# Gate and up of the last four blocks: six of eleven column groups by two levels of seven products

## The chip, the cores and the metric

One NeuronCore of a Trainium2 chip runs the whole kernel in one launch. The metric is device microseconds from start to end of the launch; the kernel before takes 1817.15 us (median of three runs, 1816.91 to 1817.16). Everything is float32. TensorE (PE in the profile) multiplies matrices into PSUM, which has eight banks of 128x512 floats; VectorE (DVE) and ScalarE (ACT) read and write PSUM and SBUF; GpSimd (POOL) works on SBUF alone here; SyncE's queue (SPq) issues nearly all DMAs, in program order.

## The reference

```python
x = x + xattn(layernorm(x), ctx, mask, mask, Wq, bq, Wk, bk, Wv, bv)   # 16 heads, per batch
n = layernorm(x)                       # x is [16, 256, 512]: 4096 rows of 512
gate = n @ lut[gate_idx].T             # 512 -> 1376
up   = n @ lut[up_idx].T               # 512 -> 1376
h    = silu(gate) * up
x    = x + h @ lut[down_idx].T         # 1376 -> 512
```

## The kernel before

The kernel has three stages: attention, then gate and up, then down. The change is in the second and at the start of the third.

**Tiling.** The 4096 rows are eight blocks of 512 rows. `xTs[n]` holds block n, normalized and turned: 512 features in four chunks of 128 by 512 rows. `wg` and `wu` hold gate and up, four chunks of 128 features by 1376 columns. The columns are eleven groups `o` of 128, the last of 96 (`NO` is 11). Two blocks make a pair `p`, 0 to 3.

**A unit** (`unit(p, o)`, L942 to L1006) makes gate and up of one column group for one pair by one level of a seven-product scheme (Winograd's form of Strassen's): the two rows of the left matrix are gate and up, its two columns the halves of the features; the two columns of the right one are the blocks of the pair. Each of the seven products, pa, pe, pa, pb, pa, pc, pd in the order of issue, is two matmuls of 128x512 (the two chunks of a half), so a unit has 14 where eight plain products would take 16. Sums that a scheme like this needs are made ahead: of the weights by `combine_w` into `sw` and in place in `wu`, of the rows by `combine_x` (L848) into `xe` and in place in `xTs`. Sums of the products are made in PSUM: ScalarE copies a bank (`copied`, L961), and later products are added onto the bank and onto its copy. Three products are joined with others by VectorE from PSUM (L989 hb, L993 w, L1003 ha); ScalarE applies Silu to `sg` (L983) and `w` (L994), GpSimd multiplies hb by w (L995), and SyncE's queue stores both parts to DRAM (`store_h`). The addition ha is put off into the next unit (`hold`).

**The order of units** (L1009) is written out: `gate_up` does column group 0 of pairs 0 and 1 plainly, then come 20 units of pairs 0 and 1 and all 22 of pairs 2 and 3. Within a unit, places are left for VectorE's other work: `hooks` run at three places of a unit (loads of rows, their statistics, normalizing, turning, `combine_x`; `turn_blocks` sets them), and `fill(ns)` adds to a budget and emits as many of the table look-ups that are still to be done (`todo`: the rest of the weights, `combine_w`, then the down weights `wd`) as fit into it, by planned costs. The fills of one unit sum to 9300 planned ns.

**Down** (`down7`, L1182) takes a block's h in four quarters, again by seven products q1 to q7 of five or six matmuls of 128x256 each, on four PSUM banks (`ps_b`). Its weight sums t2, t3, t4 and `wl` are made once, by VectorE, in `before_down` (L1097), mixed with the sums of block 0's h (`combine_h(0)`: s1, s2, an in-place difference, s4). Two steps of it run in the last unit, three after it, and one after each of the first additions of the first `down7`, where q6 needs s2 and t2, q7 needs t3, q5 needs `wl`. Every `down7` also loads two tiles of x (`load_x2`, L1188) that its second addition (L1222) and later ones need. Block 0's h is loaded in unit (3, 2), half of block 1's in unit (3, 5); the pools of the gate and up stage are then closed, and at L1236 the other half of block 1 and block 2 are loaded. For later blocks, block n + 2 is loaded when block n is done.

Of the kernel before, what the change touches and what calls it, by code (L numbers as in the profile page):

```python
# [9 lines left out]
F32 = mybir.dt.float32  # L10
I32 = mybir.dt.int32
AF = mybir.ActivationFunctionType
ALU = mybir.AluOpType
# [6 lines left out]
def kernel(  # L20
# [34 lines left out]
    nc = tc.nc  # L55
    P = 128
    B, C, T = x.shape
# [10 lines left out]
    NH = T // P  # L68
# [107 lines left out]
    xTs = {}  # L176
# [7 lines left out]
    def load_x2(k):  # L184
        x2s[k] = rpool.tile([P, T], F32, tag="x2", name=f"x2t_{k}", bufs=4)
        nc.sync.dma_start(x2s[k], x2_d[k])
        return x2s[k]
# [617 lines left out]
    with ExitStack() as ffn:  # L805
# [7 lines left out]
        )  # L813
        first = ffn.enter_context(ExitStack())
        sp = first.enter_context(tc.tile_pool(name="ffns", bufs=1))
        f1 = first.enter_context(tc.tile_pool(name="ffn1", bufs=3))

# [9 lines left out]
        def store_h(n, o, ht, rows):  # L827
            nc.sync.dma_start(hds[n][o, :rows, :], ht[:rows])
# [83 lines left out]
        def fill(ns):  # L912

            room[0] = min(room[0] + ns, 8000.0)
            while room[0] > 0:
                took, op = next(todo, (0, None))
                if op is None:
                    break
                op()
                room[0] -= took  # L920
# [21 lines left out]
        def unit(p, o, hooks):  # L942
# [27 lines left out]
            if held:  # L970
                held.pop()()
            pe = bank("pe", ps_f, "ae")
            product(pe, sw[:, 0], t1, onto=False)
            p5 = rpool.tile([P, 4 * P], F32, tag="us1", name=f"p5_{p}_{o}", bufs=1)[:rows]
            nc.scalar.copy(p5, pe)
            fill(2000)
            product(pa, sw[:, 1], xe[:, 1])
# [15 lines left out]
            v.tensor_tensor(w, pc, p5, ALU.add)  # L993
            nc.scalar.activation(w, w, AF.Silu)  # L994
            nc.gpsimd.tensor_tensor(hb, hb, w, ALU.mult)  # L995
            store_h(2 * p + 1, o, hb, rows)
            product(pd, a22, xe[:, 2])
            hooks[2]()
            fill(1700)

# [4 lines left out]

            held.append(hold)  # L1006


        order = [(p, o) for o in range(1, 8) for p in range(2)]  # L1009
        order += [(p, o) for p in range(2) for o in range(8, NO)]  # L1010
        order += [(p, o) for p in range(2, 4) for o in range(NO)]
        hooks = defaultdict(list)

        def turn_blocks(n, at):

            k = 4 * n

            def step(i):
                if i:
                    turn2(k + i - 1)  # L1020
                if i < 8:
                    norm2(k + i)
                    room[0] -= 550
                if i + 3 < 8:
                    load_x2(k + i + 3)
                if i == 8:
                    for _ in combine_x(n // 2):
                        room[0] -= 1230

            for i in range(3):  # L1030
                hooks[divmod(at - 1, 3)].append(lambda i=i: load_x2(k + i))
            for i in range(9):
                hooks[divmod(at + i, 3)].append(lambda i=i: step(i))

        turn_blocks(4, 3 * order.index((1, 8)) - 1)
        turn_blocks(6, 3 * order.index((2, 5)))
        for i in range(8):
            for n, at in ((4, 8), (6, 15)):
                hooks[at + i, 0].append(lambda k=4 * n + i: load_x2(k))
                hooks[at + i, 1].append(lambda k=4 * n + i: (stats2(k), fill(-850)))  # L1040
        for n, at in ((4, 16), (6, 23)):
            hooks[at, 0].append(lambda n=n: [fn() for fn in rstd2(n, n + 2)] and fill(-2300))
# [26 lines left out]
        for i in range(4):  # L1069
            hooks[0, min(i, 2)].append(lambda: (next(second, None), fill(-1230)))  # L1070

        def run(fns):
            for fn in fns:
                fn()
# [6 lines left out]
        lo, hi = slice(0, 2 * P), slice(2 * P, 4 * P)  # L1081
        wl, wh, wz = wd[:, 0:HO], wd[:, HO : 2 * HO], wd[:last_rows, NO - 1]
        h_parts = {}

        def load_part(n, o, t):
            full = min(t.shape[1], NO - 1 - o)
            nc.sync.dma_start(t[:, 0:full], hds[n][o : o + full].rearrange("o p t -> p o t"))
            if full < t.shape[1]:
                nc.sync.dma_start(t[:last_rows, full, :], hds[n][NO - 1, :last_rows, :])

        def part_of(t, i):
# [43 lines left out]
        for i, (p, o) in enumerate(order):  # L1135
            if p < 2 and o in (5, 8):
                while o not in ready:
                    next(todo)[1]()
            if (p, o) == (3, 2):

                h_parts[0] = [(j, xpool.tile([P, NH, 4 * P], F32, tag="xT", name=f"h0_{j}")) for j in (0, 4)]
                h_parts[0][1] = (4, h_parts[0][1][1][:, 0 : HO - 4])
                h_parts[0].append((HO, xep.tile([P, 3, 2, 4 * P], F32, tag="xe", name="h0_2")
                                   .rearrange("p a b t -> p (a b) t")))
                for part in h_parts[0]:
                    load_part(0, *part)
            if (p, o) == (3, 5):
                for _, op in todo:
                    op()
                h_parts[1] = [(0, look[:, 0:HO])]  # L1150
                load_part(1, *h_parts[1][0])
            if (p, o) == order[-1]:
                pre = before_down()
                hooks[i, 1].append(lambda: next(pre))
                hooks[i, 2].append(lambda: next(pre))
            unit(p, o, [lambda i=i, j=j: run(hooks.pop((i, j), ())) for j in range(3)])
        held.pop()()
        first.close()
        hp = ffn.enter_context(tc.tile_pool(name="ffnh", bufs=2))

        def load_high(n):
            h_parts[n].append((HO, hp.tile([P, NO - HO, 4 * P], F32, tag="hh", name=f"hh_{n}")))
            load_part(n, *h_parts[n][-1])

        def load_h(n):
            low = look[:, 0:HO] if n % 2 else hp.tile([P, HO, 4 * P], F32, tag="hl", name=f"hl_{n}", bufs=1)
            h_parts[n] = [(0, low)]
            load_part(n, 0, low)
            load_high(n)

# [11 lines left out]
        def down7(n, t, pre=iter(())):  # L1182
# [4 lines left out]
            first_t, second_t = slice(t * P, (t + 1) * P), slice((t + 2) * P, (t + 3) * P)  # L1187
            xrs = [load_x2(4 * n + t), load_x2(4 * n + t + 2)]  # L1188

# [45 lines left out]

        load_high(1)  # L1236
        load_h(2)
        for _ in range(3):
# [3 lines left out]
        for n in range(nblocks):  # L1242
            if n:
                down7(n, 0)
            if n + 1 < nblocks:
                for _ in combine_h(n + 1):
                    pass
            down7(n, 1)
            h_parts.pop(n)
            if n == 0:  # L1250
                new_e(0)
            elif n + 2 < nblocks:
                load_h(n + 2)

# [45 lines left out]
```

## Time and profile before

| | us |
|---|---|
| median of three runs | 1817.15 |
| the profiled execution | 1816.28 |
| its span, first to last instruction | 1814.5 |
| TensorE busy | 1783.5 |
| VectorE busy | 1340.0 |
| ScalarE busy | 870.8 |
| GpSimd busy | 435.8 |
| the 42 units, first to last matmul | about 1009.7 to 1525.5 |
| down | about 1525.5 to 1814.5 |

The granted TensorE clock is 0.996 of full speed over the span. A float32 matmul of this kernel shows as two matmul records. Neighbouring records overlap, so a mean duration of one (592 ns for 128x512) is longer than the time from one start to the next, and the rate of TensorE is read from starts. "Idle before" in the profile is time in which an engine had nothing to do just before an instruction, and the name behind the arrow is what ended it.

### The profile page before, as it was taken

To read this page: it belongs to the slowest core of one execution; us is meant where nothing else is said; L and a number is where in the kernel's file an instruction comes from. 1 tells how busy PE (TensorE), PEld (TensorE's weight loads), DVE (VectorE), ACT (ScalarE), POOL (GpSimd) and SP (SyncE) were. 2 spreads that over 40 slices of the span, in tenths; PEclk is the share of its full clock that TensorE was granted. 3 is DMA by queue.
4 is the path that set the end of the run, shared out by engine and by line. 5 is a ranking of instruction groups with operands and counts; after the bars stand their busy time and mean duration, and the time that the engine had idled before them with its cause. 6 is when DMAs were issued, how large, how long until landed. Compare 5 with 4: busy or idle time off the path is not lost.

```text
span 1814.5 us, 28718 instructions
## 1 busy us (share of the span) xinstructions
PE 1783.5 (98%) x10982; PEld 836.5 (46%) x10982; DVE 1340.0 (74%) x1886; ACT 870.8 (48%) x1651; POOL 435.8 (24%) x425
## 2 busy tenths in 40 slices
PE   8999999999999999999999999999999998899999
PEld 4333333333333333333344444444444444788887
DVE  6898999989998999998887788887873113453352
ACT  2777777777777777777775222233232221000000
POOL 4334333434334443444322111101111010000000
PEclk9999999999999999999999999999999999999999
DMA  6445533333434245444332111232221323233531
GB/s 188 132 145 155 155 105 125 121 116 93 127 121 128 89 127 153 143 133 123 111 103 87 60 58 68 76 119 73 70 91 38 109 75 117 69 132 125 178 132 59
DMA packets 118937, 201.09 MB, mean 111 GB/s; under 512 B 21892, under 2 KB 24072, under 8 KB 118800
## 3 DMA queue, kind: packets, MB, share of 16 engines
q1 hardware_dynamic: 114528, 196.21, 34.1%
q0 software_dynamic: 3168, 1.86, 0.5%
q8 instruction: 87, 1.43, 0.3%
q10 hardware_dynamic: 1104, 1.19, 0.2%
q14 instruction: 50, 0.41, 0.1%
HBM read 135.83 MB, written 58.10 MB: 107 GB/s over the span
## 4 chain that ended last, share of the span: by engine, by line
PE 91%; DVE 3%; DMA 2%; ACT 1%; SPq 0%; issue 0%; DVEq 0%; ACTq 0%
PE pa L490 15%; PE pv L537 12%; PE pa L956 12%; PE q L1199 12%; PE pb L498 11%; PE pb L956 4%; PE pd L956 4%; PE pc L956 4%; PE pe L956 4%; PE pv L413 3%; PE pq L413 3%; PE pk L413 3%; DMA x2t<-x 2%; PE pgu L930 2%; DVE nm L506 1%; PE q L1204 1%
## 5 line engine op out<-in xcount | busy, mean ns | idle before, releaser
L506 DVE TENSOR_REDUCE nm<-pa 128x2 f32<-128x1024 f32 x512 | 602.1, 1217 | 84.9 <-PE pb L498 79.7
L510 ACT ACTIVATE pt<-pb 128x512 f32<-128x512 f32 x1024 | 530.3, 603 | 105.9 <-PE pb L498 104.4
L490 PE MATMUL pa<-kp,qp 32*128 32x512 f32 x2048 | 514.2, 616 | 6.5 <-DVE nm L506 3.8
L498 PE MATMUL pb<-qp,kp 32*128 32x512 f32 x2048 | 517.4, 617 | 0.0
L490 PEld LDWEIGHTS pa<-kp,qp 32*128 32x128 f32 x2048 | 177.7, 184 | 200.4 <-DVE nm L506 152.8
L537 PE MATMUL pv<-pt,va 128*32 128x512 f32 x2048 | 246.2, 598 | 0.0
L498 PEld LDWEIGHTS pb<-qp,kp 32*128 32x128 f32 x2048 | 209.9, 183 | 73.2 <-issue 41.3
L995 POOL TENSOR_TENSOR hb<-hb,w 128x512 f32<-128x512 f32 (+1 forms) x42 | 57.2, 1362 | 465.4 <-ACT w L994 448.2
L989 DVE TENSOR_TENSOR hb<-pa,p 128x512 f32<-128x512 f32 (+1 forms) x42 | 29.0, 689 | 148.3 <-ACT pd L963 148.3
L537 PEld LDWEIGHTS pv<-pt,va 128*32 128x32 f32 x2048 | 53.4, 109 | 173.1 <-ACT pt L510 97.1
L1218 ACT COPY q<-q 128x256 f32<-128x256 f32 x16 | 6.0, 372 | 265.1 <-PE q L1199 265.1
L542 ACT COPY us<-pv 128x512 f32<-128x512 f32 x128 | 75.0, 586 | 94.6 <-PE pv L537 94.6
L521 POOL DMA_DIRECT2D qp<-mx x64 | 38.3, 599 | 312.5 <-DVE mx L520 295.1
L549 POOL TENSOR_TENSOR us<-us,us 128x512 f32<-128x512 f32 x64 | 82.3, 1286 | 15.1 <-ACT us L542 15.0
L956 PE MATMUL pa<-xe,sw 128*128 128x512 f32 (+1 forms) x168 | 79.9, 598 | 2.1 <-ACT pb L963 2.1
L956 PE MATMUL pb<-xT,wg 128*128 128x512 f32 (+1 forms) x168 | 79.9, 598 | 0.0
L956 PE MATMUL pc<-xT,sw 128*128 128x512 f32 (+1 forms) x168 | 79.0, 592 | 0.0
L956 PE MATMUL pa<-xT,wg 128*128 128x512 f32 (+1 forms) x168 | 78.9, 592 | 0.0
L956 PE MATMUL pd<-xe,wu 128*128 128x512 f32 (+1 forms) x168 | 78.9, 592 | 0.0
L956 PE MATMUL pa<-xe,wu 128*128 128x512 f32 (+1 forms) x168 | 78.9, 592 | 0.0
L956 PE MATMUL pe<-xT,sw 128*128 128x512 f32 (+1 forms) x168 | 78.9, 592 | 0.0
L429 POOL TENSOR_TENSOR natk<-natk,mb 128x512 f32<-128x512 f32 x31 | 40.9, 1318 | 145.9 <-ACT natk L426 140.6
(227 smaller groups left out, 2405.2 us busy)
## 6 DMA issues: line engine op xcount, KB each, us to landing
x2t<-x SPq DMA_DIRECT2D x96, 256.0 KB
kp<-kd SPq DMA_DIRECT2D x62, 256.0 KB
qp<-qd SPq DMA_DIRECT2D x62, 256.0 KB
h<-hb SPq DMA_DIRECT2D x38, 256.0 KB
h<-ha SPq DMA_DIRECT2D x38, 256.0 KB
hh<-h SPq DMA_DIRECT2D x7, 1280.0 KB
rb<-rd SPq DMA_DIRECT2D x32, 256.0 KB
xr<-in_x_dram SPq DMA_DIRECT2D x32, 256.0 KB
```

The lines of the kernel that those rows point to most:

```text
L413: nc.tensor.matmul(ps[32 * j : 32 * j + 32], weights(o, slice(first + 32 * j, first + 32 * j + 32)), moving(o), start=(o == 0), stop=(o == ...
L429: nc.gpsimd.tensor_tensor(t, t, mb, ALU.mult)
L490: nc.tensor.matmul(pa[:, jj, :], qps[ua % 4][at, ca * P : (ca + 1) * P], kps[ua % 4][at, :], start=True, stop=True,)
L498: nc.tensor.matmul(pb, kps[ub % 4][at, cb * P : (cb + 1) * P], qps[ub % 4][at, :], start=True, stop=True,)
L506: nc.vector.tensor_reduce(nms[ua][:, 2 * half : 2 * half + 2, ca], pa, AX.X, ALU.max, negate=True)
L510: nc.scalar.activation(pts[sb][:, j, :], pb, AF.Exp)
L537: nc.tensor.matmul(ps[32 * j : 32 * j + 32, :], va[:, at : at + 32], pt[:, j, :], start=(i == 0), stop=(i == 1),)
L542: nc.scalar.copy(us[u, half], ps)
L549: nc.gpsimd.tensor_tensor(a, a, b, ALU.add)
L956: nc.tensor.matmul(ps, a[:, h, at], b[:, h, :], start=h == 0 and not onto, stop=h == 1, skip_group_check=onto,)
L995: nc.gpsimd.tensor_tensor(hb, hb, w, ALU.mult)
L1199: nc.tensor.matmul(ps, a(o)[:, at], b[:, o, :], start=o == 0, stop=o == HO - 1 and not more,)
```

## The change

For pairs 2 and 3, units are left only for column groups 0, 1, 2, 3 and 10, ten units in place of 22. Column groups 4 to 9 are taken two at a time, (4, 5), (6, 7), (8, 9), for both pairs at once, by a second level of the same scheme (`quads`). For each **column pair** there are seven **items**, one for each product of the first level, in the order `seq`: 1, 2, 6, 7, 4, 3, 5. In an item, the left matrix has the two column groups and the two chunks of 128 features, the right one the two chunks and the two pairs, and it is done by seven **products** of one matmul of 128x512 each. They are issued in the order f6, f2, f5, f7, then the f1 of the next item, f3, f4. Four results of 128x512 come out of an item (for two column groups and two pairs), and each is added to running sums in SBUF.

- `second_x(i)` makes the sums of rows of item i once, four VectorE instructions of 128x512; it runs for items 1, 2, 6 ahead of the first column pair and for 7, 4, 3, 5 in items 1, 2, 6, 7 of it (`tails`).
- `second_w`, by `factors`, makes the sums of weights for each item, four instructions of 128x128, one item ahead.
- Per item ScalarE copies three banks. `share_e` reads the bank pe (one buffer) twice, `result` reads the others.
- Running sums are in buffers of tags that the units used (us0, x2, us1, rb, xr); sums of rows and the first loads of h lie in parts of `sw`, `look`, `wg` and `wu` that are no longer needed.
- In the units, Silu of w, GpSimd's multiplication and the store of hb are put off into the next unit (`hold_w`), the last fill is 2200 instead of 1700, `combine_x` is spread over two hooks, and statistics and turning of pairs 2 and 3 run earlier.
- The loads of h for blocks 0 and 1 are issued in the last column pair, together with the x tiles of block 0's two `down7`; only the low half of block 1 is loaded after it. `before_down`'s first two steps run in the last item. Block 2 is loaded after block 0 is done. `combine_h(n + 1)` runs between the additions of the second `down7` of block n rather than ahead of it.

```diff
@@ unit
             if held:
-                held.pop()()
+                held.pop(0)()
...
             nc.scalar.copy(p5, pe)
+            if held:
+                held.pop(0)()
             fill(2000)
...
             v.tensor_tensor(w, pc, p5, ALU.add)
-            nc.scalar.activation(w, w, AF.Silu)
-            nc.gpsimd.tensor_tensor(hb, hb, w, ALU.mult)
-            store_h(2 * p + 1, o, hb, rows)
             product(pd, a22, xe[:, 2])
             hooks[2]()
-            fill(1700)
+            fill(2200)
...
-            held.append(hold)
+            def hold_w():
+                nc.scalar.activation(w, w, AF.Silu)
+                nc.gpsimd.tensor_tensor(hb, hb, w, ALU.mult)
+                store_h(2 * p + 1, o, hb, rows)
+
+            held.extend([hold, hold_w])
...
-        order += [(p, o) for p in range(2, 4) for o in range(NO)]
+        order += [(p, o) for p in range(2, 4) for o in (0, 1, 2, 3, NO - 1)]
...
                 if i == 8:
-                    for _ in combine_x(n // 2):
+                    combining.append(combine_x(n // 2))
+                if i >= 8:
+                    for _ in range(2):
+                        next(combining[-1])
                         room[0] -= 1230
...
-        turn_blocks(6, 3 * order.index((2, 5)))
+        turn_blocks(6, 3 * order.index((2, 0)) - 1)
...
+        def second_x(i):
+            b1, b2 = rows_in(2, i), rows_in(3, i)
+            t2, t3, t4 = t_of[i]
+            v.tensor_tensor(t3, b2[:, 1], b2[:, 0], ALU.subtract)
+            v.tensor_tensor(b2[:, 0], b2[:, 0], b1[:, 0], ALU.subtract)
+            v.tensor_tensor(t2, b2[:, 1], b2[:, 0], ALU.subtract)
+            v.tensor_tensor(t4, b1[:, 1], t2, ALU.subtract)
...
+        def second_w(i, at, at2, ring):
+            a = weights_of(i)
+            s1, s2, s4 = (ring[:, j * P : (j + 1) * P] for j in range(3))
+            v.tensor_tensor(s1, a[:, 0, at2], a[:, 1, at2], ALU.add)
+            v.tensor_tensor(s2, s1, a[:, 0, at], ALU.subtract)
+            v.tensor_tensor(a[:, 0, at2], a[:, 0, at], a[:, 0, at2], ALU.subtract)
+            v.tensor_tensor(s4, a[:, 1, at], s2, ALU.subtract)
...
+            def begin(j, f):
+                pa = bank(j, "a")
+                product(pa, f[1], onto=False)
+                return pa, copied(j, "b", pa)
...
+                else:
+                    if shared:
+                        v.tensor_tensor(tmp, ps, tmp, ALU.add)
+                        v.tensor_tensor(r, tmp, r, ALU.add)
+                        nc.gpsimd.tensor_tensor(w, tmp, w, ALU.add)
+                    else:
+                        v.tensor_tensor(w, ps, w, ALU.add)
+                        v.tensor_tensor(r, ps, r, ALU.add)
+
+                    def end():
+                        nc.scalar.activation(w, w, AF.Silu)
+                        nc.gpsimd.tensor_tensor(r, r, w, ALU.mult)
+                        store_h(5 + 2 * pair, o, r, P)
+
+                    late.append(end)
...
+            for j, (q, o, i) in enumerate(work):
...
+                nf = factors(j + 1) if j + 1 < len(work) else None
+                product(pa, f[6])
+                pc = copied(j, "c", pa)
+                if late:
+                    late.pop(0)()
+                product(pb, f[2])
+                result(q, o, i, 0, pb, tmps[0])
+                pe = bank(j, "e")
+                product(pe, f[5], onto=False)
+                share_e(q, i, pe, tmps)
+                product(pa, f[7])
+                pd = copied(j, "d", pa)
+                if nf:
+                    na, nb = begin(j + 1, nf)
+                result(q, o, i, 1, pa, tmps[1])
+                product(pc, f[3])
+                result(q, o, i, 2, pc, tmps[2])
+                product(pd, f[4])
+                for _ in range(3):
+                    if late:
+                        late.pop(0)()
+                for fn in tails.get((q, i), ()):
+                    fn()
+                result(q, o, i, 3, pd, tmps[3])
...
+        for fn in held:
+            fn()
+        second_x(2)
+        second_x(6)
+        pre = before_down()
+        last_q = len(pairs_of_o) - 1
+        quads(extra, {
+            (0, 1): [lambda: second_x(7)], (0, 2): [lambda: second_x(4)],
+            (0, 6): [lambda: second_x(3)], (0, 7): [lambda: second_x(5)],
+            (last_q, 1): [lambda: load_high(1)], (last_q, 2): [lambda: load_high(0)],
+            (last_q, 7): [lambda: load_low(0)],
+            (last_q, 3): [lambda: xrs_of.update({(0, t): load_xrs(0, t) for t in range(2)})],
+            (last_q, 5): [lambda: next(pre), lambda: next(pre)],
+        })
...
-        load_high(1)
-        load_h(2)
+        load_low(1)
         for _ in range(3):
             next(pre)
         down7(0, 0, pre)
...
-            if n + 1 < nblocks:
-                for _ in combine_h(n + 1):
-                    pass
-            down7(n, 1)
+            pre = combine_h(n + 1) if n + 1 < nblocks else iter(())
+            down7(n, 1, pre)
+            for _ in pre:
+                pass
```

## The prediction

> **What bounds the kernel now.** I read the page first, then busy time by stage, then TensorE's waits, then the timelines where it waits.
>
> ```profile
> PE 1783.5 (98%) x10982; PEld 836.5 (46%) x10982; DVE 1340.0 (74%) x1886; ACT 870.8 (48%) x1651; POOL 435.8 (24%) x425
> ...
> PE   8999999999999999999999999999999998899999
> ...
> DVE  6898999989998999998887788887873113453352
> ```
>
> TensorE works nearly without a break, and VectorE has room only from slice 31 on: the look-ups end there. By stage (PE, PEld, DVE, ACT, POOL):
>
> ```profile
> 1009.70:1526.00 516.30, 514.21 (x1244) 227.72 (x1243) 326.97 (x582) 156.18 (x268) 56.30 (x42) 1.00 0.22 74
> 1526.00:1562.00 36.00, 23.78 (x102) 19.75 (x101) 20.91 (x25) 0.74 (x2) 0.89 (x1) 0.86 0.51 175
> 1562.00:1814.50 252.50, 248.16 (x1147) 217.01 (x1145) 102.87 (x182) 5.21 (x14) 0.00 (x0) 1.00 0.35 117
> ```
>
> The units run at TensorE's rate (2.1 us idle of 516.3); the start of down loses 12.2 of 36. The waits that do so:
>
> ```profile
> PE q L1199 <- DVE wd L1106: 9.9, 1, 9.9
> ...
> PE pa L956 <- ACT pb L963: 2.1, 1, 2.1
> ...
> PE q L1199 <- DVE wu L1105: 2.0, 1, 2.0
> ```
>
> The first is a DMA's doing:
>
> ```profile
> 1534.23 1.62 SPq L186 DMA_DIRECT2D x2t<-x  x2
> ...
> 1545.48 0.42 DVE L1211 TENSOR_TENSOR q<-q,x2t 128x256 f32<-128x256 f32 x1 [10.37 <-DMA x2t<-x]
> 1545.83 1.48 DVE L1106 TENSOR_TENSOR wd<-wd 128x1280 f32<-128x1280 f32 x1
> ...
> 1547.46 3.83 PE L1199 MATMUL q<-wd,wg 128*128 128x256 f32 x10 [9.86 <-DVE wd L1106]
> ```
>
> The x tiles queue behind three loads of h (4.2 MB, 1530.2 to 1545.4, 277 GB/s); VectorE waits for them in order, and `wl`, which q5 needs, comes behind.
>
> **Matmuls.** One unit's pa starts at 1381.27 and the next one's at 1393.29: 12.02 us for 14 matmuls, 0.859 each. Twelve units (168) become 21 items of seven (147): 21 x 0.859 = **18.0 us less**, if TensorE stays the bound. An item lasts 6.01 us, a column pair 42.1.
>
> **VectorE in the column pairs.** Joining a 128x512 PSUM bank with SBUF takes 0.69 us (hb and w, 689 and 688 ns), two SBUF operands 0.69 too (ob_xr<-ob_xr,x2t, 692). 128x256 takes 0.424; the line through both puts 128x128, which no such addition here shows, at 0.29. Bounds are 0.21 (the 128x128 copy L357) and 0.42; I take 0.29. An item then costs: `factors` 4 x 0.29 = 1.16; item 1 two results on VectorE (the rest are ScalarE copies), 2.5 in all; items 2, 6, 7, 4, 3 six, 5.3; item 5 eight, 6.7. A column pair is 2.5 + 5 x 5.3 + 6.7 = 35.7 against TensorE's 42.1: it fits. The first also bears four `second_x` (4 x 0.69 = 2.75 each): 46.7, and two more, 5.5, stand just ahead. It doesn't fit.
>
> How far VectorE may lag follows from the order. f5 of the next item overwrites the one-buffer pe, so it waits for `share_e`, 3.2 us into VectorE's item; f6 waits for s2, 0.6 into it. Time 0 is the end of the last unit's matmuls. f1 goes at once, but f6 waits for ScalarE's copy (0.2 from matmul to copy, 0.57 the copy, as for pb, pc, pd): item 1 starts at 1.7, **0.8 lost**. VectorE finishes ha at 0.9, `second_x(2)` and `(6)` at 6.7, item 1 with `second_x(7)` at 12.0, then 8.0 us an item: item 2 at 20.0, 6 at 28.0, 7 at 36.0, item 4 at 41.3. TensorE starts item 2 at 7.7, unhindered; item 6 at 13.7, where ScalarE's Silu of item 2's third result (ready at 16.6) stands ahead of the copy that f7 needs, **1.6** lost; item 7 loses **0.25** at f5 (23.0 to 23.3); item 4 loses 1.05 at f6 and 0.95 at f5; item 3 the same: **4.0**. Item 5 then starts at 43.8.
>
> **Item 5.** Its third result goes VectorE, GpSimd's addition (1.27, L995), Silu (0.63), and only then can ScalarE copy for the next item's f7. Unlagged, the third sum is ready 6.1 us into the item, GpSimd after VectorE's next addition at 8.1, Silu 8.8, copy 9.4: 0.85 later than f7 wants. In the first pair VectorE lags some 2 us more: **3.0** lost, and 0.2 from GpSimd in item 3; in the second pair I take **1.3**, with GpSimd's interference from item 4. After the third no item follows. Item 1 (2.5 us of VectorE) lets it catch up. All told **9.9 and 1.3 us back**.
>
> **GpSimd against VectorE.** An addition with both inputs in SBUF suffers when GpSimd works:
>
> ```profile
> 1524.56 2.62 DVE L1125 TENSOR_TENSOR wg<-wg,h 128x1024 f32<-128x1024 f32 x2
> ...
> 1525.49 1.40 POOL L995 TENSOR_TENSOR hb<-hb,w 96x512 f32<-96x512 f32 x1 [10.74 <-ACT w L994]
> ```
>
> The two should take 1.22 + 0.42; they take 2.62, one microsecond more. A column pair has ten GpSimd instructions (it had one per unit) against VectorE's `factors`, `second_x` and r additions. For one PSUM input, the 512 reductions L506 in attention, with GpSimd busy 38% of that time, range only from 1193 to 1233 ns, so I charge the results nothing. [...]
>
> **Start of down.** In the last item VectorE has eight results, `before_down`'s first two (1.48 each), then t2's two and the difference before q6 and q7. Without collisions q6 waits until 8.4 us after the last matmul, though q1 and q2 end at 4.75 (3.6), and q7 2.4 for t3: 6.0 idle. With GpSimd's remaining five instructions taking turns with VectorE's five, 10.4. I take 9.2, nearer the collision that the row shows. The x tiles now come three items earlier (18 us ahead, against 11.2 to land at their worst), so the 9.9 us wait goes. 12.2 becomes 9.2: **3.0 less** (1.8 to 6.2). The loads: high halves of 1.5 MB in items 1 and 2 (5.4 us each at 277 GB/s), block 0's low half three items before the end, block 1's about 8 us after it and needed some 25 us later: hidden by the matmuls of item 7 to 5 and of the first `down7`; uncovered, 5 us. Block 2 now loads between blocks as blocks 3 to 7 did, where TensorE lost nothing outside the tail.
>
> **Units.** The 2.1 us wait arose so:
>
> ```profile
> 1254.75 1.23 DVE L856 TENSOR_TENSOR xe<-xT,xe 128x1024 f32<-128x1024 f32 x1
> ...
> 1257.29 0.68 DVE L993 TENSOR_TENSOR w<-pc,p 96x512 f32<-96x512 f32 x1
> 1258.06 0.63 ACT L994 ACTIVATE w<-w 96x512 f32<-96x512 f32 x1 [7.12 <-DVE w L993]
> 1258.60 0.57 ACT L963 COPY pb<-pa 128x512 f32<-128x512 f32 x1
> ...
> 1259.22 2.83 PE L956 MATMUL pa<-xe,sw 128*128 128x512 f32 x4 [2.09 <-ACT pb L963]
> ```
>
> Four `combine_x` in one lump made w late, Silu waited, the next unit's copy behind it. With Silu held and the lump split, **2.1 less**. The held store of hb now goes out some 6 us into a unit, not 1.5, and the statistics' x loads queue behind it on SyncE: VectorE may wait about 2 us once, then lags by it, which `hold`'s slack (w must be done before p5 is written, 5 us later) covers; if not, 2 us. VectorE's look-ups must now end in 30 units: planned, 82 (eight weight pieces) + 140 (eleven of wd) + 15 (`combine_w`) + 46 (rows) - 9 (done ahead) = 274 us; at 9.3 a unit 29.5 (the trace's last look-up ends at 1369.9, unit 30), at 9.8 unit 28.0. VectorE, 10.2 of 12.0 us per unit now (42.6 of 50), goes to about 10.7. So nothing is left to flush ahead of the last unit, and these moves cost nothing.
>
> **Sum**: -18.0 + 9.9 + 1.3 - 3.0 - 2.1 = -11.9 us. The profiled execution, 1816.28 (span 1814.5 and 1.8 around it), would become 1804.4; the median lies 0.87 above it, so 1805.2, told as **1805**. With the bounds (128x128 at 0.21 or 0.42, a lag cost of 6 to 14, the start of down from 6 to 12) its own range is 1797 to 1813.
>
> **Rivals.** *VectorE hides all of it*: TensorE may run further ahead than I allow. For: two of three column pairs need only 35.7 of 42.1. Against: the one-buffer pe. Lost then are 0.8 and twice 0.85, and 6.0 in down: -18.0 + 2.5 - 6.2 - 2.1 = -23.8, 1793. Chance 0.12.
>
> *A late flush or a load that stands in the way*: look-ups left before the last unit (a piece is 12.7 planned us), or items of the last pair waiting for the loads into `sw`, which they read elsewhere (5.4 us each). For: the margin is two units. Against: the sums above. About 9 us back: 1814. Chance 0.13.
>
> *VectorE and GpSimd bound every column pair* (slower): each of the ten GpSimd instructions costs VectorE its 1.27 us, and some 50 VectorE instructions 0.1 more each for waits. Then a pair takes 35.7 + 12.7 + 5 = 53 us, the first 70 with its `second_x`: 177 against the 144.2 of twelve units, 1845; at half of the extra, about 1831. It decides from 47 us a pair on, given 55 for the first: 149 in all, which eats the gains of 5.1 elsewhere too. For: the collision shown. Against: most results have a PSUM input. Chance 0.18.
>
> **How the numbers follow.** The forecast has 0.57. The range, **1792 to 1821**, takes in the first two rivals and leaves out most of the slow one and a little below. A change within 0.2% (1813.5 to 1820.8) is about what a measurement can't tell from none. Faster: 0.57 x 0.97 + 0.12 + 0.06 = 0.73; same 0.09; slower 0.18.
>
> **What would show it.** 10940 matmul records; units without a wait on pb; first column pair near 51 us, the second 43.4, third near 42; TensorE's waits in the first on VectorE's reads of pe and on ScalarE's copies; no wait for x2t at the start of down, with idle there of 6 to 10. I am wrong if the second pair takes over 46, the first under 45, or VectorE still does look-ups in the last unit.

## The result and the profile after

The changed kernel takes **1805.62 us** (median of four runs, 1802.83 to 1807.08) against 1817.03 for the kernel before on the same chip (1816.44 to 1817.16): a ratio of 0.9936, with an interval of 0.9919 to 0.9953. Its profiled execution took 1805.71 with a span of 1803.9, 10.6 us less than before.

The page of the changed kernel, busy times and then the rows of 40 slices:

```profile
PE 1772.4 (98%) x10940; PEld 831.5 (46%) x10940; DVE 1443.4 (80%) x2079; ACT 884.0 (49%) x1684; POOL 464.0 (26%) x443
...
PE   9999999999999999999999999999999997999999
...
DVE  6898999999899989998887788988886988434343
...
PEclk9999999999999999999999999999999998999999
```

There are 42 matmul records fewer, two for each of the 21 products saved. VectorE has 193 instructions more and is now busy for 0.8 to 0.9 of slices 32 to 34, where it had room. The one slice, 34, where TensorE and its granted clock both dip is the start of down.

Busy time by stage (PE, PEld, DVE, ACT, POOL, then granted clock, DMA share, GB/s): the 30 units, then stretches of about one column pair each, then the start of down.

```profile
1005.00:1377.00 372.00, 372.00 (x915) 164.90 (x914) 303.22 (x550) 111.68 (x197) 41.41 (x30) 1.00 0.22 75
1377.00:1421.90 44.90, 42.27 (x96) 17.29 (x95) 43.85 (x82) 16.29 (x30) 6.34 (x5) 1.00 0.09 33
1421.90:1468.00 46.10, 44.01 (x100) 19.10 (x99) 40.70 (x74) 19.32 (x36) 13.60 (x10) 0.96 0.12 46
1468.00:1513.46 45.46, 44.27 (x103) 19.20 (x102) 38.30 (x66) 20.73 (x38) 13.75 (x11) 1.00 0.47 165
1513.46:1550.00 36.54, 26.09 (x97) 21.26 (x96) 24.80 (x25) 2.63 (x5) 11.98 (x6) 0.77 0.23 79
```

The units have no gap left. In the first column pair VectorE is busy 43.85 of 44.90: there it is the bound. Of these five stretches, the second pair (0.96) and the start of down (0.77) have a granted clock below 1.00. TensorE's longest waits after the units:

```profile
PE q L1379 <- DVE wg L1292: 8.5, 1, 8.5
PE qa L1150 <- ACT qc L1154: 3.5, 3, 2.1
PE q L1379 <- DVE wu L1294: 2.0, 1, 2.0
PE qa L1150 <- ACT qb L1154: 1.3, 2, 0.7
```

I cut the column pairs where the first product f1 of a pair starts, so that each stretch holds a whole number of products (47, 49 and 51 of 0.859 us); what a stretch has above these is lost.

| | predicted | measured |
|---|---|---|
| 21 products fewer | -18.0 | -18.0 |
| first pair to the next f1: VectorE's lag | +6.9 | 44.84 - 40.37 = +4.5 |
| item 5 of the first pair, and what follows | +3.0 | 46.12 - 42.09 = +4.0 |
| item 5 of the second pair, and what follows | +1.3 | 45.48 - 43.81 = +1.7 |
| the wait in the units | -2.1 | -4.05 (from e1_units) |
| start of down | -3.0 | 290.44 - 289.03 = +1.4 |
| ahead of the units | 0 | -0.2 |
| sum | -11.9 | -10.6 |

The forecast was 1805 us. The total came out close partly by luck: two misses have opposite signs, as the pairs and units gave 2.9 more than forecast and the start of down 4.4 less. What the clock took also differs between executions (the last section): e0_after, the same kernel profiled again, has a span of 1799.1.

### The profile page after: what moved, and what is told of

It reads as the page before. It is cut to its first block, busy times and chain, and to the rows that moved or that the text cites. A ratio compares the mean times of both kernels' runs of the same rounds, so it can differ in the third digit from the quotient of the medians.

```text
span 1803.9 us, 28920 instructions
## 1 busy us (share of the span) xinstructions
PE 1772.4 (98%) x10940; PEld 831.5 (46%) x10940; DVE 1443.4 (80%) x2079; ACT 884.0 (49%) x1684; POOL 464.0 (26%) x443
## 4 chain that ended last, share of the span: by engine, by line
PE 90%; DVE 5%; DMA 1%; ACT 1%; issue 1%; POOL 0%; SPq 0%; ACTq 0%; DVEq 0%
PE pa L490 15%; PE pv L537 12%; PE q L1379 12%; PE pb L498 11%; PE pa L955 9%; PE pv L413 3%; PE pq L413 3%; PE pk L413 3%; PE pc L955 3%; PE pb L955 3%; PE pe L955 3%; PE pd L955 3%; PE qa L1150 2%; PE pgu L929 2%; PE q L1384 1%; DVE nm L506 1%
## 5 line engine op out<-in xcount | busy, mean ns | idle before, releaser
L1006 POOL TENSOR_TENSOR hb<-hb,w 128x512 f32<-128x512 f32 (+1 forms) x30 | 42.7, 1422 | 331.6 <-ACT w L1005 310.4
L1391 DVE TENSOR_TENSOR qw<-q,q 128x256 f32<-128x256 f32 x16 | 6.8, 425 | 101.7 <-PE q L1379 101.7
L962 ACT COPY pb<-pa 128x512 f32<-128x512 f32 (+1 forms) x30 | 17.1, 569 | 123.5 <-PE pa L955 123.5
L156 DVE TENSOR_SCALAR look<-look,lut_x,lut_b 128x512 int32<-128x512 int32 (+2 forms) x133 | 73.4, 581 | 0.5
L429 POOL TENSOR_TENSOR natq<-natq,mb 128x512 f32<-128x512 f32 x31 | 41.2, 1329 | 115.4 <-ACT natq L428 96.0
L413 PE MATMUL pv<-wv,ctx 128*32 128x256 f32 x1024 | 68.3, 385 | 0.9 <-ACT pt L510 0.9
L413 PE MATMUL pq<-xn,wq 128*32 128x512 f32 x496 | 59.8, 599 | 0.6 <-POOL va L457 0.6
L413 PE MATMUL pk<-ctx,wk 128*32 128x512 f32 x496 | 59.6, 598 | 0.0
L160 DVE COPY_PREDICATED look<-look 128x512 int32<-128x512 int32 (+2 forms) x76 | 56.5, 744 | 2.0
```

The costliest lines, as they stand in the source:

```text
L156: v.tensor_scalar(to, m[0], a, c, ALU.bitwise_and, ALU.bitwise_xor)
L413: nc.tensor.matmul(ps[32 * j : 32 * j + 32], weights(o, slice(first + 32 * j, first + 32 * j + 32)), moving(o), start=(o == 0), stop=(o == ...
L429: nc.gpsimd.tensor_tensor(t, t, mb, ALU.mult)
```

## The experiments

All kernels below but e1_units differ from the changed kernel, called *after*, by the edit shown. They ran later, on two chips where the kernel before took 1815.0 to 1823.7, and the first unit of these kernels begins anywhere from 1009.3 to 1013.5 us. Stages are therefore compared, not totals: the three stretches (44.84, 46.12, 45.48 in after) and the length of down (290.44). "Measured" gives the total first, then the three stretches, then down. Most runs are one execution. The 30 units took 367.51 or 367.52 in every one of them.

**e1_units**: the kernel before with the held Silu and the split `combine_x` alone; its fills and the order of its units stay.

```diff
-                held.pop()()
+                held.pop(0)()
...
+            if held:
+                held.pop(0)()
...
+            def hold_w():
+                nc.scalar.activation(w, w, AF.Silu)
...
-                    for _ in combine_x(n // 2):
+                    combining.append(combine_x(n // 2))
+                if i >= 8:
+                    for _ in range(2):
+                        next(combining[-1])
```

> The kernel before with the held Silu and the split combine_x alone (no column pairs, fills and orders as before). Stage of the units in the kernel before: one gap of 2.09 us in TensorE, after which eight records start 2.62 us apart per four instead of 1.72. Theory, that a gap costs its own length and then some 1.8 us at a lower clock: 3.9 us less, 1813.2. Rival, that only the gap counts: 2.1 us less, 1815.0. Rival, that the gap moves to another wait: no change.

The granted clock behind the wait in before (third from the end), then, in e1_units, the product that took 2.83 there:

```profile
1259.00:1264.00 5.00, 4.78 (x7) 2.03 (x8) 3.22 (x5) 1.26 (x3) 1.29 (x1) 0.66 0.54 167
```

```profile
1257.46 1.88 PE L956 MATMUL pa<-xe,sw 128*128 128x512 f32 x4
```

Measured: the 42 units took 511.72, against 515.77 in the profile of before: 4.05 less. The wait removed was 2.09. The other 2 us are in the records behind that wait in the profile of before: two groups of four took 2.83 and 2.78, where e1_units has 1.88, and the clock granted over 1259.0 to 1264.0 was 0.66. So the clock theory holds for this stage. The totals do not tell the kernels apart: 1816.76 (1812.66 to 1820.27, ten runs) against 1818.17, ratio 0.9992 (0.9977 to 1.0007); down was 290.79, with 10.6 of waiting before q5, for x2t as in before.

**e2_vadd**: item 5's two additions on GpSimd go to VectorE.

```diff
                         v.tensor_tensor(tmp, ps, tmp, ALU.add)
+                        v.tensor_tensor(w, tmp, w, ALU.add)
                         v.tensor_tensor(r, tmp, r, ALU.add)
-                        nc.gpsimd.tensor_tensor(w, tmp, w, ALU.add)
```

> The changed kernel with the two GpSimd additions of item 5 on VectorE, ahead of its r addition. Theory, that the chain VectorE, GpSimd, Silu, ScalarE's copy makes f7 of the following item 1 late: the waits of 2.09 and 1.20 us at the start of the second and third column pair go, with the slow clock after the first, and the second pair (from f1 to f1) falls from 46.1 to about 42.2 us, the third by 1.3; the whole 1800 to 1801. Rival, that VectorE's own lag makes f7 late: two more instructions of 0.7 us there make the waits longer, and the second pair takes 46 to 48.

For this run and the next, the wait behind item 5 of the first pair as it is in after (timeline: start, duration):

```profile
1424.59 3.48 POOL L1197 TENSOR_TENSOR acc_us<-tmp,acc_us 128x512 f32<-128x512 f32 x2 [6.75 <-DVE tmp L1195]
...
1428.10 0.63 ACT L1203 ACTIVATE acc_us<-acc_us 128x512 f32<-128x512 f32 x1 [1.06 <-POOL acc_us L1197]
1428.63 0.58 ACT L1154 COPY qc<-qa 128x512 f32<-128x512 f32 x1
...
1429.27 1.43 PE L1150 MATMUL qa<-sw,wg 128*128 128x512 f32 x2 [2.09 <-ACT qc L1154]
...
1430.49 1.91 PE L1150 MATMUL qa<-xT,wg 128*128 128x512 f32 x2
```

GpSimd ends its second addition at 1428.07, ScalarE's Silu at 1428.10 was waiting for it, and the copy that TensorE wants stands behind that Silu. In e2_vadd:

```profile
1426.10 1.27 POOL L1204 TENSOR_TENSOR acc_us<-acc_us,acc_us 128x512 f32<-128x512 f32 x1 [6.28 <-ACT acc_us L1203]
...
1426.53 1.39 DVE L1196 TENSOR_TENSOR acc_us<-tmp,acc_us 128x512 f32<-128x512 f32 x1
...
1428.66 1.26 POOL L1204 TENSOR_TENSOR acc_us<-acc_us,acc_us 128x512 f32<-128x512 f32 x1 [1.29 <-ACT acc_us L1203]
...
1429.15 1.32 DVE L1196 TENSOR_TENSOR acc_us<-tmp,acc_us 128x512 f32<-128x512 f32 x1
...
1430.51 0.63 ACT L1203 ACTIVATE acc_us<-acc_us 128x512 f32<-128x512 f32 x1 [1.93 <-DVE acc_us L1196]
...
1431.04 0.58 ACT L1154 COPY qc<-qa 128x512 f32<-128x512 f32 x1
...
1431.67 1.19 PE L1150 MATMUL qa<-sw,wg 128*128 128x512 f32 x2 [2.51 <-ACT qc L1154]
```

Measured: 1806.07; 44.86, 46.53, 46.28. The wait grew from 2.09 to 2.51. VectorE's additions of two SBUF operands take 1.39 and 1.32 instead of 0.69 while GpSimd multiplies next to them (1.27 and 1.26). The times are those of the rival (46 to 48). But the copy again stands behind a Silu that waits, now for VectorE, so this run rules out GpSimd's addition as the cause and leaves open whether VectorE's lag or the place in ScalarE's queue is it.

**e3_pop2**: the additions stay on GpSimd, but in item 5 ScalarE's third Silu is issued behind the next item's copy.

```diff
-                for _ in range(3):
+                for _ in range(2 if i == 5 else 3):
```

> The changed kernel with only two of the waiting Silu put into ScalarE's queue at the end of item 5, so that the third stands behind the next item's first copy. Theory, that the place in ScalarE's queue is what makes f7 late: both waits go and the time is 1800 to 1801, as without the GpSimd additions. Rival, that f7 waits for VectorE or GpSimd itself: both waits stay at 2.1 and 1.2.

```profile
1427.47 0.58 ACT L1154 COPY qc<-qa 128x512 f32<-128x512 f32 x1
1428.10 1.12 PE L1150 MATMUL qa<-sw,wg 128*128 128x512 f32 x2 [0.40 <-ACT qc L1154]
...
1428.63 0.63 ACT L1203 ACTIVATE acc_us<-acc_us 128x512 f32<-128x512 f32 x1 [0.58 <-POOL acc_us L1197]
```

Measured: 1799.91; 44.85, 42.81, 44.03; down 288.88. The waits of 2.09 and 1.20 became 0.40 and none, with GpSimd as slow as before (3.49 for its two additions). What cost time was the order in ScalarE's queue: a Silu that waits holds up a copy whose input is ready. The 0.40 left is behind the second Silu, which still stands ahead of the copy. The second stretch now exceeds its 49 products by only 0.72, the third its 51 by 0.22.

**e4_busy**: matmuls whose result nobody reads fill TensorE's gaps at the start of down, so that only the clock changes.

```diff
+            if n == 0 and t == 0:
+                keep_busy(9)
             add(w, product(6, lambda o: s2[:, o], first_t, t2), p1)
+            if n == 0 and t == 0:
+                keep_busy(2)
             add(p1, p1, xrs[0][:, lo])
```

> The changed kernel with nine matmuls (identity by a row of wd, 128x512, result unused) between q2 and q6 of the first down7 and two between q6 and q7, where TensorE waits 8.5 and 2.0 us. Theory, that TensorE's clock falls in the gap and costs 5.3 us after it: the ten records of q6 and of q7 take 2.3 us each in place of 4.6, and the whole is 4 to 5 us shorter, about 1801. Rival, that q6 and q7 are slow from what they read, or that VectorE sets the time in any case: q6 stays at 4.6, and the time at 1805 to 1806.

First the same place in after, VectorE's four steps of `before_down`, GpSimd's multiplications and TensorE's q6 and q7:

```profile
1515.57 2.58 DVE L1310 TENSOR_TENSOR wg<-look,sw 128x1280 f32<-128x1280 f32 x1
...
1516.77 4.99 POOL L1204 TENSOR_TENSOR acc_us<-acc_us,acc_us 128x512 f32<-128x512 f32 x2
1518.19 2.44 DVE L1314 TENSOR_TENSOR wg<-wg,look 128x1280 f32<-128x1280 f32 x1
...
1521.74 2.57 DVE L1291 TENSOR_TENSOR wg<-wd 128x1280 f32<-128x1280 f32 x1
...
1524.35 2.43 DVE L1292 TENSOR_TENSOR wg<-wg,wd 128x1280 f32<-128x1280 f32 x1
...
1526.84 4.63 PE L1379 MATMUL q<-wg 128*128 128x256 f32 x10 [8.46 <-DVE wg L1292]
...
1533.46 4.64 PE L1379 MATMUL q<-wu,look 128*128 128x256 f32 x10 [1.99 <-DVE wu L1294]
```

And in e4_busy, TensorE alone:

```profile
1519.77 7.89 PE L1405 MATMUL busy<-wd,ident 128*128 128x512 f32 x18
1528.43 2.42 PE L1379 MATMUL q<-wg 128*128 128x256 f32 x10 [0.77 <-DVE wg L1292]
1530.69 1.88 PE L1405 MATMUL busy<-wd,ident 128*128 128x512 f32 x4
1532.84 2.43 PE L1379 MATMUL q<-wu,look 128*128 128x256 f32 x10 [0.27 <-DVE wu L1294]
```

The start of down in e4_busy, with the granted clock third from the end:

```profile
1515.02:1550.00 34.98, 33.94 (x134) 25.08 (x133) 24.64 (x25) 2.63 (x5) 12.01 (x6) 1.00 0.24 83
```

Measured: 1802.00; 44.85, 44.42, 45.48; down 285.18, 5.3 less than in after. q6 starts no earlier (13.4 us into down, as in after), but q6 and q7 take 2.42 and 2.43 in place of 4.63 and 4.64; with q5 they account for 5.0 of the 5.3. The work added is useless, and it makes the stage shorter: the loss behind the gaps is the clock's. This is one execution, but in all six profiles with the gap of 8.5 to 8.7 before q6 (after, e0_after, e2_vadd, e3_pop2, e6_tails, e11_latex) q6 takes 3.90 to 4.63 and down 287.5 to 290.6.

**e5_nopool**: GpSimd's six instructions of item 5 in the last pair are left out.

```diff
-                        nc.gpsimd.tensor_tensor(w, tmp, w, ALU.add)
+                        if q < 2:
+                            nc.gpsimd.tensor_tensor(w, tmp, w, ALU.add)
...
-                        nc.gpsimd.tensor_tensor(r, r, w, ALU.mult)
+                        if q < 2:
+                            nc.gpsimd.tensor_tensor(r, r, w, ALU.mult)
```

> The changed kernel with GpSimd's six instructions in item 5 of the last column pair left out: the two additions onto w and the four multiplications by Silu, so that the second half of h of column groups 8 and 9 is wrong for pairs 2 and 3. Theory, that VectorE's 128x1280 additions at the start of down are lengthened by taking turns with GpSimd: they take 1.48 us in place of 2.4 to 2.6, and TensorE's wait before q6 falls from 8.5 to 4 us (my sum without collisions: 3.6), that before q7 stays near 2.0 to 2.4. Rival, that q6 waits for the loads of h: 8 to 8.5 us as before.

```profile
1516.04 1.49 DVE L1312 TENSOR_TENSOR wg<-look,sw 128x1280 f32<-128x1280 f32 x1
...
1521.68 1.49 DVE L1294 TENSOR_TENSOR wg<-wg,wd 128x1280 f32<-128x1280 f32 x1
...
1523.23 3.80 PE L1381 MATMUL q<-wg 128*128 128x256 f32 x10 [4.01 <-DVE wg L1294]
```

Measured: 1799.79; 44.85, 46.12, 45.48; down 283.70. VectorE's steps take 1.49 instead of 2.43 to 2.58; q6 waits 4.01 instead of 8.46, q7 1.99 as before. That is 6.0 idle with no collision and 10.45 with it. The loads of h are the same, so q6 did not wait for them.

**e6_tails**: in the first pair, `second_x` comes behind the fourth result of its item, so that the running sums come first.

```diff
+                if q:
+                    for fn in tails.get((q, i), ()):
+                        fn()
                 result(q, o, i, 3, pd, tmps[3])
+                if not q:
+                    for fn in tails.get((q, i), ()):
+                        fn()
```

> The changed kernel with second_x in the first column pair put behind the item's fourth result, not ahead of it. The stretch from the first f1 to the second pair's f1 takes 44.84 us, 4.5 over the 47 products. Theory, that VectorE's order makes the fourth result late, and through it ScalarE's Silu and the bank of the next copy (waits of 0.5 and 0.7 on ScalarE): these two go, the stretch takes 43 to 43.7. Rival, that the sum of VectorE's work there decides, as I predicted: 44.5 to 45, since the sum is the same.

Measured: 1804.11; the first stretch is 44.84, as in after. The waits only moved, in part to `factors` (0.63 and 0.44 on L1115). In the first pair the order of VectorE's work does not count. That its sum does is the rival's forecast and fits; no run took work out of that sum.

**e7_early**: four steps of `before_down` are emitted in item 3 of the last pair, ahead of item 5's additions.

```diff
             (last_q, 3): [lambda: xrs_of.update({(0, t): load_xrs(0, t) for t in range(2)})]
+            + [lambda: next(pre)] * 4,
-            (last_q, 5): [lambda: next(pre), lambda: next(pre)],
...
-        for _ in range(3):
+        for _ in range(1):
             next(pre)
```

> The changed kernel with the first four steps of before_down (s1, s2 and both of t2) in item 3 of the last column pair, one item earlier, in place of two in item 5 and two after it. Theory, that VectorE's chain behind the last item sets the start of down: q6 waits under 1 us in place of 8.5, q7 waits 4 to 6 (for p1's copy and t3), and down takes 281 to 285 us in place of 290.4. Rival, that VectorE is full there and the work only moves: items 3 and 5 get as much longer as down gets shorter.

```profile
1528.35 0.37 ACT L1398 COPY q<-q 128x256 f32<-128x256 f32 x1 [4.64 <-DMA h<-acc_us]
...
1530.63 4.32 PE L1379 MATMUL q<-wu,look 128*128 128x256 f32 x10 [6.25 <-DVE wu L1294]
```

Measured: 1801.84; 44.85, 44.42, 46.94; down 282.90. The wait of q6 is gone, q1 waits 1.30 for a result's addition, the third stretch is 1.46 longer, and q7 now waits 6.25: ScalarE's copy p1 goes to a buffer (tag us1) that a store of h still reads, and VectorE's q7 step is queued behind the addition that needs p1. Still a gain of 6.1 over stretch and down together against after, and of 3.1 against e0_after, which lost less to the clock.

**e8_all**: the edits of e3_pop2, e6_tails and e7_early together.

```diff
+                for _ in range(2 if i == 5 else 3):
...
+                if not q:
+                    for fn in tails.get((q, i), ()):
...
+            + [lambda: next(pre)] * 4,
```

> The changed kernel with e3, e6 and e7 together. If their gains add: 5 us from ScalarE's order, 1 from the order of second_x, 7 from the start of down, 1792 to 1794 by the changed kernel's 1805.6. Rival, that they share one resource, VectorE, and take from each other: 1797 to 1800.

Measured: 1794.76; 44.85, 42.82, 45.49; down 282.42. By stage the gains add up: 11.3 against after, where e3_pop2 had 4.8 in the column pairs, e6_tails none and e7_early 6.1. The third stretch is e3_pop2's 44.03 and the 1.46 of e7_early. The wait of 6.2 before q7 stays.

**e0_after**: the changed kernel once more, on the chip of the next three runs.

> The changed kernel again, on the same chip as the next three: 1803 to 1807 by its first runs. Theory, that its spread comes from where the clock recovers after the two gaps at the start of down: down's length differs between profiles of the same code by up to 3 us (290.4, 288.9, 287.6 so far), the column pairs' by under 0.5.

Measured: 1803.70 (1800.88 to 1806.35, four runs), ratio to before 0.9919 (0.9901 to 0.9937). The profile has the waits of after to 0.02 us, but stretches of 44.83, 44.44, 45.48 and a down of 287.50. Its q6 and q7:

```profile
1524.97 4.63 PE L1379 MATMUL q<-wg 128*128 128x256 f32 x10 [8.45 <-DVE wg L1292]
1531.59 2.43 PE L1379 MATMUL q<-wu,look 128*128 128x256 f32 x10 [1.98 <-DVE wu L1294]
```

Against after's 4.63 and 4.64, the same code with the same waits loses 2.2 us to the clock where after lost 5.0 (q6, q7 and 0.65 in q5). The theory fits for down. That the column pairs differ by under 0.5 is not: the second stretch is 1.7 shorter than in after. The two together, 2.9 and 1.7, are nearly all of the 4.8 us between the two profiled executions.

**e9_p1**: e3_pop2, all `second_x` behind the fourth result, every step of `before_down` that preceded the first `down7` in the last pair, and p1 of the first `down7` in a free buffer.

```diff
+                for _ in range(2 if i == 5 else 3):
...
+            + [lambda: next(pre)] * 4,
+            (last_q, 5): [lambda: next(pre)] * 2,
...
-            p1 = tile_of("us1", "q1", 1)
+            p1 = tile_of(*(("us1", "q1", 1) if n or t else ("xn2", "q1", 2)))
```

> e8 with three things more: before_down's third and fourth pair of steps (the difference for q7 and t3) in item 5, second_x and all of these behind the item's fourth result, and q1's copy of the first down7 in a buffer of its own (tag xn2), since in e8 it waited 4.64 us for the store of the buffer that it shares. Theory, that this store is what q7 waited for: the wait of 6.2 us before q7 falls to about 2.5, the 1.3 at q1 goes, the clock loss halves, 1788 to 1791. Rival, that VectorE's turns with GpSimd set it anyway: 5 to 6 us stay, 1793 to 1795.

```profile
1515.85 3.75 POOL L1204 TENSOR_TENSOR acc_us<-acc_us,acc_us 128x512 f32<-128x512 f32 x2
1515.86 2.61 DVE L1317 TENSOR_TENSOR look<-look 128x1280 f32<-128x1280 f32 x1
...
1518.40 2.54 DVE L1294 TENSOR_TENSOR wu<-wd 128x1280 f32<-128x1280 f32 x1
...
1520.99 3.99 PE L1380 MATMUL q<-wu,look 128*128 128x256 f32 x10 [4.20 <-DVE wu L1294]
```

Measured: 1794.28 (1792.05 to 1798.11, four runs), ratio to before 0.9875 (0.9856 to 0.9893); 44.82, 42.78, 44.03; down 281.18. The wait for p1's buffer is gone. q7 still waits 4.20, where 2.5 was expected: two steps now run beside GpSimd's multiplications and take 2.61 and 2.54 instead of 1.48. The 1788 to 1791 expected was missed; the time is that of the rival, VectorE's turns with GpSimd.

**e10_p1busy**: e9_p1 with two matmuls whose result nobody reads in the gap before q7.

```diff
+            if n == 0 and t == 0:
+                keep_busy(2)
             add(p1, p1, xrs[0][:, lo])
```

> e9 with two matmuls without use (identity by a row of wd) between q6 and q7 of the first down7. Theory, that a gap over 2 us lowers the clock for the next records and one under 1 us doesn't: q7's ten records in 2.3 us in place of 4, 1 to 2 us less than e9. Rival, that the gap of e9 is too short to matter: the same as e9 within 0.5 us.

Measured: 1792.92 (1791.26 to 1794.08), ratio 0.9860 (0.9845 to 0.9874); down 281.86. A gap of 2.49 was left, and q7 still took 4.07. The added matmuls show no gain here, and this kernel can't be told from e9_p1. As the gap did not fall under 1 us, the half of the theory that speaks of such gaps was not put to the test. These two are the fastest, 0.5 and 0.6% ahead of the changed kernel on the same chip.

**e11_latex**: the x tiles of block 0 are loaded inside `down7`, as before the change.

```diff
-            (last_q, 3): [lambda: xrs_of.update({(0, t): load_xrs(0, t) for t in range(2)})],
```

> The changed kernel with the x tiles of block 0's down7 loaded where the kernel before loads them, in down7, behind the load of block 1's low half. Theory of the prediction, that loading them three items earlier is what took the wait of 9.9 us away: VectorE waits 5 us or more for x2t, and q5 some 4 us for wl. Rival, that 1.3 MB ahead of them in place of 4.2 MB is what did it: they land about 7 us after block 1's load is issued, VectorE gets to them at about the same time, and TensorE waits under 1 us more.

```profile
1527.12 1.02 SPq L186 DMA_DIRECT2D x2t<-x  x2
...
1534.20 0.42 DVE L1390 TENSOR_TENSOR q<-q,x2t 128x256 f32<-128x256 f32 x1
```

Measured: 1806.61; down 290.58, as in after. The tiles are issued late and used 7.1 us later without a wait: issuing them early is not what removed the 9.9 us wait of before. Two things are left that could have removed it. 1.3 MB of h is queued ahead of the tiles, in place of 4.2 MB; and VectorE comes to them 7.1 us after they are issued, since q6 is late, where in before it stood idle for them 0.9 us after (1545.48 less 10.37, against 1534.23). No run parts the two.

## Why the prediction was right, point by point

**The signs.** The prediction named a first pair under 45 or a second over 46 as signs of being wrong, and the stretches of 44.84 and 46.12 look like both. But its figures (43.4 is 42.1 and the 1.3) count the loss behind item 5 to the pair that the item ends, and the stretches above count it to the next. With the measured losses, counted that way, the first pair takes 42.1 + 4.5 + 4.0 = 50.6, where 51 was forecast, and the second 42.1 + 1.7 = 43.8, where 43.4 was.

**Products.** 42 records fewer, at 0.859 a product: as worked out.

**VectorE's lag in the first pair.** Mechanism right, size too large: 4.5 against 6.9. Items 2, 6, 7 and 4 ended on VectorE 18.9, 26.2, 33.5 and 38.0 us after the last unit's matmuls, where I had 20.0, 28.0, 36.0 and 41.3. I had counted additions by their duration, 0.69 and 0.29. In the trace, independent ones start 0.60 to 0.61 apart at 128x512 and 0.20 at 128x128, so an item is shorter by a tenth. The losses also lie elsewhere than forecast: each wait with the 0.1 us by which the product behind it is slower, about 0.5 at f7 of item 6 (1.6 forecast), 0.8 at its f4 (none), 0.3 in item 4 (2.0), 1.3 in item 3 (2.0) and 0.7 at f5 of item 5 (none). The last follows two of item 5's `factors` that took 1.24 and 1.35 us beside GpSimd, in place of 0.28; the prediction had 0.2 for GpSimd in item 3, where they run.

**Item 5.** The chain (VectorE, GpSimd, Silu, then the copy) is what the trace shows, and 3.0 and 1.3 were near the 4.0 and 1.7. e2_vadd and e3_pop2 say which link mattered: not GpSimd's speed but the place of the third Silu in ScalarE's queue. Of the 4.0, 1.7 is clock, which the prediction did not price: e0_after, with the same wait, lost 2.35. So 3.0 was too much for the wait and too little for the wait with the clock, and that it lies between is luck.

**Units.** The step "Silu held and the lump split" was right: no wait on pb is left, and the look-ups were done in time (the last ends at 1348.0, and VectorE idles 8.55 us ahead of 1362.4). I had priced the wait at its length, 2.1. Here it was worth 4.05, as it took the slow records behind it away too.

**Start of down: the step that failed.** "12.2 becomes 9.2: 3.0 less" became 1.4 more. Two parts are wrong. The idle time is 10.45, not the 9.2 that I took between 6.0 and 10.4: the two bounds are what was measured, with GpSimd (10.45) and without (6.0, e5_nopool). Beside GpSimd's instructions VectorE's four steps of 128x1280 took 2.43 to 2.58, in e5_nopool, where those are left out, 1.48 to 1.49. The 10.4 supposed that the two engines take whole turns, which no trace shows as such; the row of before had one microsecond more beside an instruction of 1.40. Taking the bound rather than a value near it would have been right. The larger part is the clock, which the prediction put at nothing on both sides. Before, 9.9 of the 12.2 was one gap late in the stage with 1.5 us of slow records behind it (ten records of q5 took 3.83 instead of 2.32). After, gaps of 8.46 and 1.99 frame q6, and 5.0 us of slow records follow. e4_busy filled the gaps, these records ran at full speed (2.42 for ten of q6, 2.43 for ten of q7), and down became 5.3 shorter. As e0_after lost only 2.2 there, some 3 us of the size is this execution's; with that, down is 1.5 shorter than before, still short of the 3.0 forecast.

**The x tiles.** That their wait is gone was right, the reason (loaded three items earlier) was not: loaded late, they are not waited for either (e11_latex).

**The rivals.** That VectorE hides everything (1793) failed in the first pair, where it is busy 43.85 of 44.90. A late flush or load (1814): no wait on either shows. VectorE and GpSimd as the bound of every pair (slower from 149 us on): three pairs took 136.4. VectorE's additions with an input in PSUM took 0.68 to 0.69 beside GpSimd too; only those of two SBUF operands were longer (behind item 5 of the first pair 1.25 to 1.39 at 128x128, instead of 0.28 to 0.29), and in a pair few of them meet GpSimd's ten instructions.

## What to carry to other kernels

A gap in TensorE's work is priced by its length and by what runs at a lower clock behind it, here up to 5 us for gaps of 8.5 and 2.0; the records' durations just behind a gap show it (ten records in 4.63 instead of 2.42). On an engine that works in order, as ScalarE did here (its copy at 1428.63 ran behind the Silu of 1428.10, which had waited 1.06), put an instruction that may wait behind the copy that TensorE needs, even where its wait looks short: one place in ScalarE's queue was worth about 1.5 us in each of two column pairs, and 3.3 where the clock fell too. Where a VectorE instruction with two SBUF operands meets GpSimd, count the time it takes there (here 2.43 to 2.58 us instead of 1.48 at 128x1280, 1.25 to 1.39 instead of 0.28 to 0.29 at 128x128), or move it to where GpSimd rests.

## What the runs showed that I had not expected

**The same gap does not always cost the same.** The wait of 2.09 to 2.11 us behind the first pair's item 5 was in every run of this order of item 5. The second stretch (the row by stage, granted clock third from the end) in after, and then in e0_after:

```profile
1421.86:1467.98 46.12, 44.03 (x100) 19.12 (x99) 40.74 (x74) 19.34 (x36) 13.60 (x10) 0.96 0.12 46
```

```profile
1421.68:1466.12 44.44, 42.33 (x100) 18.54 (x99) 40.39 (x74) 19.25 (x36) 13.62 (x10) 1.00 0.13 48
```

It was 46.12 in after and e5_nopool, and 44.42 to 44.44 in e0_after, e4_busy, e6_tails, e7_early and e11_latex: 1.7 us or nothing. Down with the same order of work took 287.5 to 290.6. This is of the size of the spread of the changed kernel's runs (4.2 us on the first chip, 5.5 on e0_after's). The kernel before spread by 0.7 on the first chip but by 5.7 on the other, so a wide spread is not the change's alone. Behind the same wait the granted clock was 0.64 in after (1429.2 to 1434.0) and 1.00 in e0_after (1427.4 to 1432.0); behind the gap of 8.46 in after it was 0.50 (1526.8 to 1534.0). A gap of 2.09 to 2.11 was thus enough in some executions and not in others, and what decides it no run shows.
